# Graph attention stack on one core: a product moved to ScalarE as a biased exponential, the first norm written one step sooner, start and end rearranged

## The chip, the core and the metric

The kernel runs on one core of one Trainium2 chip. The engines of the core work from queues of their own, each in order: TensorE (PE in the profile, PEld for its weight loads), VectorE (DVE), ScalarE (ACT), GpSimd (POOL) and SyncE (SP, which here only issues DMA transfers). They wait for each other by semaphores. The metric is the time of one execution on the device in microseconds (us), as the median of several runs; the profile is of one further execution.

## The reference

The input `x` holds 32 batches of 512 nodes with 256 features, in float32; `adj` is a 512 x 512 adjacency matrix shared by all batches. Four layers follow, each added to its input:

- every layer starts with `h = max((x - mean) / sqrt(var + 1e-5), 0)` along the features;
- layers 0 and 1 are graph attention with one head: `Wh = h W`, `e_ij = leaky_relu(s_i + s_j)` masked by `adj`, softmax along j, the average of `Wh` with these weights, then elu (layer 0) or relu (layer 1);
- layer 2 is the same with four heads of 64 features;
- layer 3 is a linear map to 512 features, an attention over all nodes without a mask, a linear map back to 256, and a masked attention, with elu twice and residuals.

Since `leaky_relu(z) = max(z, alpha z)`, its exponential is the maximum of two products of a factor of i and a factor of j, so the kernel needs exponentials of the vectors `s_i` and `s_j` alone, and one maximum per pair of nodes.

## The kernel before

**Streams.** Four streams work on the batches in turn; stream i takes batches i, i+4, i+8 and so on. Each is a Python generator (`batch`, `layer0` to `layer3`) that yields the moment at which it wants to be taken up again, and the loop at the end of `fast` always continues the generator that is due first. That sets the order in which instructions are written. `after_us` computes the due time from TensorE work and a given number of us. The framework's planner then orders the written instructions on every engine, with an earlier written one going first where several are ready by its own timing; `keep_in_program_order` ties an instruction behind the one written before it on its engine. The order on each engine is fixed once the program runs.

**The norm** (`norm`, L262). For two blocks of 128 nodes: BN_STATS and BN_AGGR on VectorE (L268, L269), Ln of the variance and Exp of -0.5 times it on ScalarE (L271, L272), which gives `rs`, 1/deviation. Then VectorE writes `xn`: either the full norm (L279, `late` false: the first norm of a batch and that ahead of layer 3) or only `x` minus the mean (L275, ahead of layers 1 and 2), where `rs` is multiplied in behind the projection. `batch` (L729) takes a batch's tile, which was loaded a batch earlier, does the first norm on its four blocks, yields, and begins layer 0. `turned` (L291) transposes `xn` on TensorE (L70) and ScalarE copies it out with relu (L289). All streams share three `xn` buffers.

**The values** (`values`, L307). Per block of 128 nodes two matmuls (L66) give 256 features and 3 attention columns in a PSUM bank. In layers 0 and 3 ScalarE takes Exp of the 3 columns (L318) and then writes the features times the first of these (L319). In layer 1, with `rs`, ScalarE takes Exp of the columns scaled by `rs` (L321), VectorE multiplies `rs` with the first of them into `both` (L323), and ScalarE writes the features times `both` (L324), which frees the bank. While all streams are active a stream has two banks of its own.

**The weights** are written on VectorE (L352, one instruction per block of nodes), aggregation is matmuls of them with the values. Layer 3 avoids the full matrix for its unmasked attention by sorting: a scatter by indirect DMA (L606, issued by GpSimd), running sums on VectorE and TensorE (L626 to L647), and a gather (L654). The last batch does that attention directly instead (`attend`).

**The output step** (`layer3`, from L694): for two blocks at a time Exp and Relu of the averages (L698, L699), a second elu (L409 to L411), transposes of the residual, a sum (L709), Relu (L710), the sum with `x` on GpSimd (L712) and the store (L713).

**The start.** SyncE issues the load of the first `x`, then W0 and its attention vectors `a0`, `adj` fifth, and the rest. The vectors are scaled on VectorE (`scale_a`, L109), W0 is completed by three columns (`project`, copies at L126). `setup` turns `adj` into a mask: `own` (L209, L210), transposes, `maskT` (L219). A minimum over `adj` (L225), for a test of whether the fast form may be used, is written after that.

Of the kernel before, what the change touches and what calls it, by code (L numbers as in the profile page):

```python
# [28 lines left out]
P = 128  # L29
# [6 lines left out]
def fast(ctx, tc, flag, x, adj, w0, a0, w1, a1, w2, a2, mlp1_w, mlp1_b, mlp2_w, mlp2_b,  # L36
# [70 lines left out]
        return t  # L107

    def scale_a(t, alpha):  # L109
        nc.vector.tensor_scalar_mul(t[:, :, 1:2], t[:, :, 0:1], alpha - 1.0)  # L110
        nc.vector.tensor_scalar_mul(t[:, :, 2:3], t[:, :, 2:3], 1.0 - alpha)

    def project(dst, block, k, a_cols):

# [13 lines left out]
    def fetch_w(w, a, name):  # L128

        kt, cols = w.shape[0] // P, w.shape[1]  # L130
        t = const.tile([P, kt, cols + 3], FP, name=name)
        wr = w.rearrange("(k p) f -> p k f", p=P)
        for c in range(0, cols, F):
            nc.sync.dma_start(t[:, :, c + (3 if c else 0):c + (3 if c else 0) + F], wr[:, :, c:c + F])
        return t, fetch_a(a, name + "a")

    def finish_w(fetched, alpha):
        t, a_cols = fetched
# [8 lines left out]
            yield  # L147


    xts = {0: load_x(0)}  # L150
    W0, _ = fetched0 = fetch_w(w0, a0, "W0")
    adj_sb = work.tile([P, NT, N], I32, tag="w", name="adj", bufs=4)
    nc.sync.dma_start(adj_sb, adj.rearrange("(t p) j -> p t j", p=P))
    for b in range(1, NS):
# [51 lines left out]
    def setup():  # L206

        own = work.tile([P, NT, N], FP, tag="w", name="own", bufs=4)
        nc.vector.tensor_scalar(own, adj_sb, 0.0, None, op0=OP.is_gt)  # L209
        nc.gpsimd.affine_select(  # L210
            out=own, in_=own, pattern=[[P, NT], [-1, N]], base=0, channel_multiplier=1,
            compare_op=OP.not_equal, fill=1.0,
        )
        for j in range(NT):
            turn[0] = NS - 1 - j % (NS - 1)
            p = bank()
            for t in range(NT):
                transpose(p[:, t * P:(t + 1) * P], own[:, t, j * P:(j + 1) * P], ident, j + t == 0)
            nc.scalar.copy(maskT[:, j, :], p)  # L219
        turn[0] = NS - 1  # L220
        yield
        yield from finish_w(fetched1, 0.01)


        tc.keep_in_program_order(nc.vector.tensor_reduce(differ[:, 0:1], adj_sb, AX.XY, OP.min))  # L225
        nc.vector.tensor_scalar(differ[:, 0:1], differ[:, 0:1], 0.0, None, op0=OP.is_lt)
        least = small([1], "rden")
        nc.vector.tensor_reduce(least, diag, AX.X, OP.min)
        nc.vector.tensor_scalar(differ[:, 1:2], least, 0.0, None, op0=OP.is_le)
        nc.vector.tensor_copy(W2[:, :, :, :D], raw2.rearrange("p k (h d) -> p k h d", d=D))  # L230
        nc.vector.tensor_scalar_mul(A2v[:, :, 1:2], A2v[:, :, 0:1], -0.8)
        nc.vector.tensor_scalar_mul(A2v[:, :, 2:3], A2v[:, :, 2:3], 0.8)
        for k in range(KF):
            project(W2[:, k, :, D:], lambda k, f: raw2[:, k, f * P:(f + 1) * P], k, A2)
            yield
        yield from finish_w(fetched3, 0.2)

        for tri, sign in ((before, 1), (after, -1)):
            nc.vector.memset(tri, 1.0)
            nc.gpsimd.affine_select(  # L240
                out=tri, in_=tri, pattern=[[sign, P]], base=0, channel_multiplier=-sign,
                compare_op=OP.is_gt, fill=0.0,
            )
        ties = work.tile([P, 2 * N - P], FP, tag="w", name="ties", bufs=4)
        nc.vector.memset(ties, TINY)
        nc.gpsimd.affine_select(
            out=ties, in_=ties, pattern=[[-1, 2 * N - P]], base=N - P, channel_multiplier=1,
            compare_op=OP.is_gt, fill=0.0,
        )
        nc.vector.tensor_copy(band, ties)  # L250
        yield
        yield from finish_w(fetched4, 0.2)

    def small(shape, name):
        return work.tile([P] + shape, FP, tag=name, name=name, bufs=2 * NS)

    def new_xn():
        return work.tile([P, NT, F], FP, tag="xn", name="xn", bufs=3)  # L260

    def norm(xt, xn, rs, t0, late):  # L262


        st = small([2, 6], "st")
        mv = small([2, 2], "mv")
        for i in range(2):
            nc.vector.bn_stats(st[:, i, :], xt[:, t0 + i, :])  # L268
            nc.vector.bn_aggr(mv[:, i, :], st[:, i, :])  # L269
        rp = rs[:, t0:t0 + 2]  # L270
        nc.scalar.activation(rp, mv[:, :, 1], AF.Ln, bias=eps)  # L271
        nc.scalar.activation(rp, rp, AF.Exp, scale=-0.5)  # L272
        for i in range(2):
            if late:
                nc.vector.tensor_scalar(  # L275
                    xn[:, t0 + i, :], xt[:, t0 + i, :], mv[:, i, 0:1], None, op0=OP.subtract
                )
            else:
                nc.vector.tensor_scalar(  # L279
                    xn[:, t0 + i, :], xt[:, t0 + i, :], mv[:, i, 0:1], rp[:, i:i + 1], op0=OP.subtract, op1=OP.mult  # L280
                )
# [22 lines left out]
        c = next(noted)  # L304
        nc.vector.tensor_reduce(seen[:, c:c + 1], e, AX.XY, OP.max)

    def values(hT, w, rs=None):  # L307

        v = work.tile([P, NT, F + 3], FP, tag="v", name="v", bufs=4)
        for t in range(NT):  # L310
# [9 lines left out]
            else:  # L320
                nc.scalar.activation(v[:, t, F:], ps[:, F:F + 3], AF.Exp, scale=rs[:, t:t + 1])  # L321
                both = small([1], "both")
                nc.vector.tensor_tensor(both, rs[:, t:t + 1], pj, op=OP.mult)  # L323
                nc.scalar.activation(v[:, t, :F], ps[:, :F], AF.Copy, scale=both)  # L324
            if t + 1 < NT:
                yield after_us(0)
# [59 lines left out]
        nc.vector.reciprocal(r, den)  # L386
        return r

    def plain(hT, w, rs=None):
        v = yield from values(hT, w, rs)  # L390
        wt = weights(lambda t: v[:, t, F + 2:F + 3], lambda j: v[:, j, F + 1:F + 2])
        note(v[:, :, F:])
        yield after_us(3.2)
# [19 lines left out]
    def layer0(xt, xn, rs, when):  # L413
        v, wt = yield from plain((yield from turned(xn, when)), W0)
        xn, rs = new_xn(), small([NT], "rs")
        for t0 in range(0, NT, 2):
            r, q = pair(), pair("q")
            for i in range(2):
# [3 lines left out]
                if i == 0:  # L422
                    yield after_us(0)
            add_elu(xt[:, t0:t0 + 2, :], r, q)
            norm(xt, xn, rs, t0, True)
            last, when = when, after_us(6)
            if t0 == 0:
                yield after_us(0)
        yield last
        return xn, rs, when  # L430

    def layer1(xt, xn, rs, when):
        v, wt = yield from plain((yield from turned(xn, when)), W1, rs)
        xn, rs = new_xn(), small([NT], "rs")
        for t0 in range(0, NT, 2):
            r = pair()
# [252 lines left out]
    def layer3(xt, xn, when, b):  # L689
# [1 line left out]
        yield from (attend if b >= B - 1 else sort_attend)(oT, b)  # L691
        rT = yield from linear_t(oT, WM2, b2, "rT", 2)
        v, wt = yield from plain(rT, WHA)
        for t0 in range(0, NT, 2):  # L694
            y, q = pair(), pair("q")
            for i in range(2):
                p, rd = averages(v, wt, t0 + i)
                nc.scalar.activation(q[:, i, :], p, AF.Exp, scale=rd)  # L698
                nc.scalar.activation(y[:, i, :], p, AF.Relu, scale=rd)  # L699
                yield after_us(0)  # L700
            elu2_plus1(y, q)
            p = bank()
            for i in range(2):
                for k in range(KF):
                    transpose(
                        p[:, (i * KF + k) * P:(i * KF + k + 1) * P], rT[:, k, (t0 + i) * P:(t0 + i + 1) * P], ident
                    )
            yf = y.rearrange("p a f -> p (a f)")
            nc.vector.scalar_tensor_tensor(yf, p, -1.0, yf, op0=OP.add, op1=OP.add)  # L709
            nc.scalar.activation(y, y, AF.Relu)  # L710
            xr = xt[:, t0:t0 + 2, :]
            nc.gpsimd.tensor_tensor(xr, xr, y, op=OP.add)  # L712
            nc.sync.dma_start(  # L713
                out[b, t0 * P:(t0 + 2) * P, :].rearrange("(t p) f -> p t f", p=P), xr
            )
            yield after_us(0)

    def mlp_in(oT, y, t):
# [7 lines left out]
            o, p.rearrange("p (f c) -> p f c", c=P), -1.0, o, op0=OP.add, op1=OP.add  # L726
        )

    def batch(b):  # L729
        xt = xts.pop(b)  # L730
        xn, rs = new_xn(), small([NT], "rs")
        for t0 in range(0, NT, 2):
            norm(xt, xn, rs, t0, False)
        yield after_us(4)
        when = after_us(2)
        for layer in (layer0, layer1, layer2):
            xn, rs, when = yield from layer(xt, xn, rs, when)
# [479 lines left out]
```

## Time and profile before

| what | value |
|---|---|
| median of 3 runs | 2943.76 us (2943.12 to 2945.2) |
| the profiled execution's own time | 2945.59 us |
| its span, first to last instruction | 2943.9 us |
| mean granted TensorE clock | 0.995 |
| bytes moved by DMA | 270.89 MB |
| period of a batch in the middle of the run | 89.3 us |

In the lines below a group of a timeline reads: start and duration in us, engine, line of the kernel, operation, what it writes <- what it reads (buffer numbers left out), partitions x elements, number of instructions; in brackets how long the engine had been idle and what ended that. A line of the waits reads: who waited <- for whom, us in total, times, the longest. A line of a group reads: line, engine, operation, operands, count | us busy, mean ns of one | us idle before it and what ended that. A line of windows gives the busy time of each engine in that stretch.

### The profile page before, as it was taken

What the parts mean: (1) busy time and instruction counts of PE and PEld (TensorE: products, weight loads), DVE (VectorE), ACT (ScalarE), POOL (GpSimd) and SP (SyncE); (2) the same over time, 40 slices, a digit from 0 to 9 for tenths busy, and PEclk for the clock granted to TensorE, in tenths of its full rate; (3) what the DMA queues carried; (4) which work ended last, traced back from release to release, by engine and by line L of the source; (5) the groups of instructions that cost most, each with busy time, mean ns of one, the idle gap of its engine ahead of it and who ended that gap; (6) DMA issues with size and microseconds to landing.
All of it is one profiled execution on the core that took longest, in us unless ns stands there. A gap on an engine that the chain in (4) does not pass through costs nothing.

```text
span 2943.9 us, 43065 instructions
## 1 busy us (share of the span) xinstructions
PE 2863.2 (97%) x15177; PEld 2326.1 (79%) x15177; DVE 2224.0 (76%) x5674; ACT 1537.4 (52%) x3918; POOL 501.3 (17%) x509
## 2 busy tenths in 40 slices
PE   7999999999999999999999999999999999999988
PEld 6777888877887877888878888778888788887766
DVE  4677877778877778878777878777777788787764
ACT  4444455554555554555554555545555555555544
POOL 0011112111122111122021121121221111221120
PEclk9999999999999999999999999999999999999999
DMA  3033223233223233233332232332232322332230
GB/s 94 19 101 99 87 83 116 92 96 99 90 87 105 95 98 98 83 102 98 98 101 90 86 107 93 96 99 89 87 116 89 99 95 81 101 112 77 96 106 23
DMA packets 193150, 270.89 MB, mean 92 GB/s; under 512 B 16992, under 2 KB 156062, under 8 KB 192928
## 3 DMA queue, kind: packets, MB, share of 16 engines
q1 hardware_dynamic: 163168, 169.76, 18.5%
q0 software_dynamic: 29760, 98.30, 10.1%
q8 instruction: 123, 2.02, 0.3%
q14 instruction: 99, 0.81, 0.1%
HBM read 152.62 MB, written 115.39 MB: 91 GB/s over the span
## 4 chain that ended last, share of the span: by engine, by line
PE 77%; DVE 13%; ACT 5%; DMA 3%; issue 1%; POOL 0%; SPq 0%; POOLq 0%; ACTq 0%; DVEq 0%
PE b L66 70%; PE b L70 7%; DVE st L268 3%; DVE xn L279 1%; DMA order<-v,at 1%; DVE xn L275 1%; DVE sums L640 1%; DVE w L352 1%; ACT v L324 1%; DMA sums<-order 1%; DVE sums L631 1%; ACT y L504 1%; DVE x L405 1%; ACT q L503 1%; DVE y L404 1%
## 5 line engine op out<-in xcount | busy, mean ns | idle before, releaser
L66 PE MATMUL b<-v,w 128*128 128x65 f32 (+1 forms) x7232 | 1222.4, 321 | 6.8 <-DVE w L352 6.7
L66 PEld LDWEIGHTS b<-v,w 128*128 128x128 f32 x7232 | 1053.6, 192 | 167.8 <-issue 64.2
L66 PE MATMUL b<-WFC,oT 128*128 128x256 f32 (+1 forms) x2048 | 496.3, 380 | 0.0
L66 PEld LDWEIGHTS b<-WFC,oT 128*128 128x128 f32 x2048 | 373.6, 189 | 48.7
L66 PE MATMUL b<-W,hT 128*128 128x259 f32 (+1 forms) x1536 | 382.0, 387 | 9.2 <-ACT hT L289 4.4
L352 DVE SCALAR_TENSOR_TENSOR w<-b,v,maskT 128x512 f32<-128x512 f32 x512 | 369.0, 743 | 4.9 <-PE b L70 3.6
L606 POOL DMA_INDIRECT order<-v,at x248 | 284.2, 1146 | 491.2 <-DVE oT L725 152.0
L66 PEld LDWEIGHTS b<-W,hT 128*128 128x128 f32 x1536 | 283.0, 190 | 58.9 <-ACT v L324 8.9
L352 DVE SCALAR_TENSOR_TENSOR w<-spread,v,maskT 128x512 f32<-128x512 f32 x384 | 269.3, 741 | 0.0
L386 DVE RECIPROCAL rden<-b 128x1 f32<-128x1 f32 (+1 forms) x516 | 78.7, 164 | 246.5 <-PE b L66 243.2
L712 POOL TENSOR_TENSOR x<-x,y 128x512 f32<-128x512 f32 x64 | 81.3, 1270 | 1074.9 <-ACT y L710 963.8
L66 PE MATMUL b<-hT,WM 128*128 128x512 f32 x512 | 248.6, 596 | 0.7 <-ACT hT L289 0.7
L654 POOL DMA_INDIRECT g<-table,at x124 | 120.9, 975 | 724.8 <-ACT y L674 385.3
L66 PE MATMUL b<-oT,WM 128*128 128x512 f32 x512 | 230.3, 592 | 0.0
L528 ACT ACTIVATE v<-b,ends 128x256 f32<-128x256 f32 x256 | 118.6, 466 | 176.7 <-PE b L66 172.4
L268 DVE BATCH_NORM_STATS2 st<-x 128x6 f32<-128x256 f32 x512 | 192.7, 408 | 5.1 <-DMA x<-in_x_dram 2.6
L289 ACT ACTIVATE hT<-b 128x512 f32<-128x512 f32 x256 | 147.0, 590 | 83.8 <-PE b L70 83.8
L338 ACT ACTIVATE oT<-b,bias 128x512 f32<-128x512 f32 x128 | 87.7, 685 | 193.2 <-PE b L66 193.2
L411 DVE TENSOR_TENSOR y<-q,y 128x512 f32<-128x512 f32 x192 | 132.5, 690 | 67.0 <-ACT q L410 66.5
L70 PE MATMUL b<-ident,xn 128*128 128x128 f32 x1024 | 152.7, 279 | 23.5 <-DVE xn L279 20.9
L66 PEld LDWEIGHTS b<-oT,WM 128*128 128x128 f32 x512 | 97.0, 190 | 95.1 <-issue 91.8
L70 PEld LDWEIGHTS b<-ident,xn 128*128 128x128 f32 x1024 | 121.9, 143 | 60.6 <-DVE xn L279 33.8
(142 smaller groups left out, 3738.3 us busy)
## 6 DMA issues: line engine op xcount, KB each, us to landing
table<-sums SPq DMA_DIRECT2D x62, 1032.0 KB
sums<-order SPq DMA_DIRECT2D x62, 516.0 KB
spread<-row SPq DMA_DIRECT2D x96, 256.0 KB
x<-in_x_dram SPq DMA_DIRECT2D x32, 512.0 KB
out_dram<-x SPq DMA_DIRECT2D x64, 256.0 KB
sums<-order SPq DMA_DIRECT2D x62, 129.0 KB
order<-v,at POOLq DMA_INDIRECT x248
g<-table,at POOLq DMA_INDIRECT x124
```

What stands on the lines that cost most here:

```text
L66: nc.tensor.matmul(p, w, x, **flags)
L70: instruction = nc.tensor.transpose(p, x, i)
L268: nc.vector.bn_stats(st[:, i, :], xt[:, t0 + i, :])
L289: nc.scalar.activation(hT[:, :, t0 * P:(t0 + 2) * P], p.rearrange("p (k n) -> p k n", k=KF), AF.Relu)
L338: nc.scalar.activation(o[:, f, :], p, AF.Relu, bias=bias[:, f:f + 1])
L352: w = nc.vector.scalar_tensor_tensor(wt[:, j, :], r, t_col(j), maskT[:, j, :], op0=OP.max, op1=OP.mult)
L386: nc.vector.reciprocal(r, den)
L411: nc.vector.tensor_tensor(r, q, r, op=OP.add)
L528: nc.scalar.activation(halves[c][:, t, :F], ps[:, :F], AF.Copy, scale=ends[:, t, 0:1])
L606: nc.gpsimd.indirect_dma_start(out=orders[c], out_offset=bass.IndirectOffsetOnAxis(ap=at[:, 0, t:t + 1], axis=0), in_=halves[c][:, t, :], ...
L654: nc.gpsimd.indirect_dma_start(out=g, out_offset=None, in_=table, in_offset=bass.IndirectOffsetOnAxis(ap=at[:, 1, t:t + 1], axis=0),)
L712: nc.gpsimd.tensor_tensor(xr, xr, y, op=OP.add)
```

## The change

It has five parts.

- `values` in layer 1: `both` is no longer a product on VectorE but an Exp on ScalarE, of the first column scaled by `rs` with `ln` as its bias; `ln` is the logarithm of `rs`. For it `norm` in layer 0 keeps the Ln in a tile of its own, and GpSimd multiplies this by -0.5 in place, two columns at a time.
- The first norm of batch b + 4 is written in the output step of batch b, after its first pair of blocks, instead of after that step. Batches 0 to 3 have theirs at the start as before.
- The last batch does its output step with one block at a time instead of two, and its sum with `x` on VectorE; its stores are of one block each.
- At the start the two loads of `a0` are issued ahead of `x` and W0; the scaling of all attention vectors is on GpSimd; the minimum over `adj` and the test behind it are written directly behind `own`, tied there.
- The buffers of `st` go from eight to four.

```diff
     def scale_a(t, alpha):
-        nc.vector.tensor_scalar_mul(t[:, :, 1:2], t[:, :, 0:1], alpha - 1.0)
-        nc.vector.tensor_scalar_mul(t[:, :, 2:3], t[:, :, 2:3], 1.0 - alpha)
+        nc.gpsimd.tensor_scalar_mul(t[:, :, 1:2], t[:, :, 0:1], alpha - 1.0)
+        nc.gpsimd.tensor_scalar_mul(t[:, :, 2:3], t[:, :, 2:3], 1.0 - alpha)
...
+    a0_sb = fetch_a(a0, "W0a")
     xts = {0: load_x(0)}
-    W0, _ = fetched0 = fetch_w(w0, a0, "W0")
+    W0, _ = fetched0 = fetch_w(w0, a0_sb, "W0")
     adj_sb = work.tile([P, NT, N], I32, tag="w", name="adj", bufs=4)
     nc.sync.dma_start(adj_sb, adj.rearrange("(t p) j -> p t j", p=P))
...
             compare_op=OP.not_equal, fill=1.0,
         )
+        tc.keep_in_program_order(nc.vector.tensor_reduce(differ[:, 0:1], adj_sb, AX.XY, OP.min))
+        nc.vector.tensor_scalar(differ[:, 0:1], differ[:, 0:1], 0.0, None, op0=OP.is_lt)
         for j in range(NT):
...
         yield from finish_w(fetched1, 0.01)
 
-        tc.keep_in_program_order(nc.vector.tensor_reduce(differ[:, 0:1], adj_sb, AX.XY, OP.min))
-        nc.vector.tensor_scalar(differ[:, 0:1], differ[:, 0:1], 0.0, None, op0=OP.is_lt)
...
-    def norm(xt, xn, rs, t0, late):
-        st = small([2, 6], "st")
+    def norm(xt, xn, rs, t0, late, ln=None):
+        st = small([2, 6], "st", NS)
...
         rp = rs[:, t0:t0 + 2]
-        nc.scalar.activation(rp, mv[:, :, 1], AF.Ln, bias=eps)
-        nc.scalar.activation(rp, rp, AF.Exp, scale=-0.5)
+        lp = rp if ln is None else ln[:, t0:t0 + 2]
+        nc.scalar.activation(lp, mv[:, :, 1], AF.Ln, bias=eps)
+        nc.scalar.activation(rp, lp, AF.Exp, scale=-0.5)
+        if ln is not None:
+            nc.gpsimd.tensor_scalar_mul(lp, lp, -0.5)
...
                 nc.scalar.activation(v[:, t, F:], ps[:, F:F + 3], AF.Exp, scale=rs[:, t:t + 1])
                 both = small([1], "both")
-                nc.vector.tensor_tensor(both, rs[:, t:t + 1], pj, op=OP.mult)
+                nc.scalar.activation(
+                    both, ps[:, F:F + 1], AF.Exp, scale=rs[:, t:t + 1], bias=ln[:, t:t + 1]
+                )
                 nc.scalar.activation(v[:, t, :F], ps[:, :F], AF.Copy, scale=both)
...
         v, wt = yield from plain(rT, WHA)
-        for t0 in range(0, NT, 2):
-            y, q = pair(), pair("q")
-            for i in range(2):
+
+        n = 1 if b == B - 1 else 2
+        for t0 in range(0, NT, n):
+            y, q = pair()[:, :n, :], pair("q")[:, :n, :]
+            for i in range(n):
...
-            xr = xt[:, t0:t0 + 2, :]
-            nc.gpsimd.tensor_tensor(xr, xr, y, op=OP.add)
+            xr = xt[:, t0:t0 + n, :]
+            (nc.gpsimd if n == 2 else nc.vector).tensor_tensor(xr, xr, y, op=OP.add)
             nc.sync.dma_start(
-                out[b, t0 * P:(t0 + 2) * P, :].rearrange("(t p) f -> p t f", p=P), xr
-            )
+                out[b, t0 * P:(t0 + n) * P, :].rearrange("(t p) f -> p t f", p=P), xr
+            )
+            if t0 == 0 and b + NS < B:
+                first_norm(b + NS)
             yield after_us(0)
...
-    def batch(b):
+    normed = {}
+
+    def first_norm(b):
+
         xt = xts.pop(b)
         xn, rs = new_xn(), small([NT], "rs")
         for t0 in range(0, NT, 2):
             norm(xt, xn, rs, t0, False)
-        yield after_us(4)
+        normed[b] = xt, xn, rs
+
+    def batch(b):
+        if b < NS:
+            first_norm(b)
+            yield after_us(4)
+        else:
+            yield after_us(4)
+        xt, xn, rs = normed.pop(b)
         when = after_us(2)
```

## The prediction

> **What bounds the kernel now.** I read the page's busy times first, then TensorE's waits from 280 to 2760 us, then the timeline around each kind of wait.
>
> ```profile
> PE 2863.2 (97%) x15177; PEld 2326.1 (79%) x15177; DVE 2224.0 (76%) x5674; ACT 1537.4 (52%) x3918; POOL 501.3 (17%) x509
> ```
>
> TensorE is busy 2863.2 of 2943.9 us and the change takes no matmul away, so it can win only from the 80.7 us of TensorE idleness. By 100 us windows about 24 of them lie before 200 us and 23 after 2800. Between, this is nearly all:
>
> ```profile
> PE b L70 <- DVE xn L279: 16.4, 28, 1.0
> PE b L70 <- ACT v L324: 12.4, 28, 0.9
> PE b L66 <- ACT v L324: 3.4, 15, 0.3
> PE b L66 <- ACT v L318: 0.8, 1, 0.8
> ```
>
> 28 waits for L279, one per batch 4 to 31 and 89.3 us apart, are the first norm of a new batch; the L324 waits are layer 1's values held back by `both`.
>
> **Part 1, first norm a step sooner.**
>
> ```profile
> 1615.47 0.17 DVE L386 RECIPROCAL rden<-b 128x1 f32<-128x1 f32 x1 [0.68 <-PE b L66]
> 1618.93 0.17 DVE L386 RECIPROCAL rden<-b 128x1 f32<-128x1 f32 x1 [3.28 <-PE b L66]
> ...
> 1626.64 1.51 DVE L279 TENSOR_SCALAR xn<-x,mv,rs 128x256 f32<-128x256 f32 x4
> ...
> 1627.11 0.77 PE L70 MATMUL b<-ident,xn 128*128 128x128 f32 x4 [0.80 <-DVE xn L279]
> ```
>
> Today its VectorE work, some 3.3 us (four statistics, four aggregates, four L279), runs just as TensorE wants it, behind layer 1's norm. It is now written after the first half of the output step, whose L712 ran at 1616.10. In 1615 to 1620 VectorE is busy 0.70 of 5.00 us, so the work falls into a hole; nothing that TensorE waits for today is queued there. The input tile was loaded a period before (L95 at 1537.87). The step issues no DMA; in ScalarE's queue two short Ln and two Exp move with it, past that step's L698 and L699. The `xn` buffer is held some 10 us longer, but of its three buffers I count two in use at 1617 to 1629, this one included. Behind the transposes TensorE has ready WFC matmuls. Of 16.4 us I take **15**; ends 8 (half turns into another wait) and 16.4.
>
> **Part 2, `both` on ScalarE.**
>
> ```profile
> 1773.63 0.27 ACT L321 ACTIVATE v<-b,rs 128x3 f32<-128x3 f32 x1
> ...
> 1775.96 0.15 DVE L323 TENSOR_TENSOR both<-rs,v 128x1 f32<-128x1 f32 x1
> 1776.15 0.47 ACT L324 ACTIVATE v<-b,both 128x256 f32<-128x256 f32 x1 [0.17 <-DVE both L323]
> ...
> 1776.68 0.65 PE L70 MATMUL b<-ident,v 128*128 128x128 f32 x4 [0.90 <-ACT v L324]
> 1776.82 0.48 DVE L631 SCALAR_TENSOR_TENSOR sums<-sums,T 128x258 f32<-128x258 f32 x1
> 1777.35 0.70 PE L66 MATMUL b<-sums,after 128*128 128x258 f32 x2
> ```
>
> The product takes 0.15 us but queues on VectorE for 2 us here; over 128 tiles paired in order L324 starts 1.86 us after L321 at the median, 0.48 at the least. L324 also frees the PSUM bank for which TensorE waits. The whole wait is not won: the matmul behind needs L631, which ends at 1777.30, and VectorE is busy 4.67 of 5.00 us in 1595 to 1600 and all of 1600 to 1605, the same place in another period. Taking 128 x 0.145 = 18.6 us off VectorE moves this by some tenths a batch. Of 16.4 us (15.8 in the view and one wait of 0.5 at 259) I take **8**; ends 0 (VectorE is late next) and 16.4.
>
> The price on ScalarE: one more activation per tile.
>
> ```profile
> L321 ACT ACTIVATE v<-b,rs 128x3 f32<-128x3 f32 x128 | 33.1, 258 | 43.2 <-PE b L66 42.8
> L318 ACT ACTIVATE v<-b 128x3 f32<-128x3 f32 x256 | 43.3, 169 | 68.1 <-PE b L66 66.7
> ```
>
> The row nearest is L321, 0.258 us with one per-partition operand; L318 without one takes 0.169. The new one has two (scale `rs`, bias `ln`), so 0.258 + 0.089 = 0.35 us. The Trainium skill ("ScalarE: Activation LUTs", What ACT_TABLE_LOAD costs) puts some 93 ns on each such operand over 186 ns, an estimate of 0.37, with 93 ns of overlap between neighbours. It speaks against the change where VectorE is free: L321 to L324 becomes about 0.26 - 0.09 + 0.35 + 0.03 = 0.55 us, above today's least. By the row 128 x 0.35 = 45 us come onto ScalarE, by the rule 48, on an engine idle for 48% of the span: **0** on the path by either, since the median wait falls by 1.3 us. Without that cover each would cost its 0.25 us net, 32 us.
>
> The `ln` multiply goes to GpSimd: 64 at 0.19 us by the row L575 (128x8), 12 us, bounded below by nothing. The skill ("GPSIMD Engine Reference", Key points) says GpSimd and VectorE share their SBUF interfaces. The trace shows it: at 1623.80 two L275 take 1.43 us beside L712, where they take 0.72 otherwise. By the durations alone these multiplies cost 0; by the rule up to 12 us of held VectorE, of which a small part meets a wait of TensorE: I take **-1**; ends 0 and -4. What is behind one in GpSimd's queue is a scatter L606 or L712; were it late, the sort's sums and the output would follow.
>
> **Part 3, the start.**
>
> ```profile
> 23.47 2.28 DVE L225 TENSOR_REDUCE differ<-adj 128x1 f32<-128x2048 int32 x1
> 25.66 2.72 DVE L352 SCALAR_TENSOR_TENSOR w<-b,v,maskT 128x512 f32<-128x512 f32 x4
> ...
> 26.46 2.94 PE L66 MATMUL b<-v,w 128*128 128x257 f32 x6 [2.73 <-DVE w L352]
> ```
>
> L225 stands straight ahead of the first weights. Moved behind `own` (10.99 to 12.22) it falls into VectorE's idle time from 12.35 to 16.35: up to +2.2. If it gets ahead of the two W0 copies at 12.13, TensorE's first projection (12.43) loses 2 instead. In SyncE's queue the two `a0` loads pass x and W0: two issues of 0.49 us, so x lands near 5.4 instead of 4.4, and the first transposes are later, unless their tiny packets hold x up more. Against that `W0a`, landed at 6.96 and 8.32, no longer stops VectorE (1.02 and 0.75 us) and its scaling leaves that queue for GpSimd, which is idle till 12.29. `adj` is still issued fifth. The scaling of the other weights is off the path. I take **+2**; ends -2 and +4.
>
> **Part 4, the end.**
>
> ```profile
> 2931.90 0.17 DVE L386 RECIPROCAL rden<-b 128x1 f32<-128x1 f32 x1
> ...
> 2932.58 1.26 POOL L712 TENSOR_TENSOR x<-x,y 128x512 f32<-128x512 f32 x1 [11.57 <-ACT y L710]
> 2932.89 1.23 DVE L409 TENSOR_SCALAR q<-q 128x512 f32<-128x512 f32 x1 [0.17 <-ACT q L698]
> ...
> 2937.20 1.26 POOL L712 TENSOR_TENSOR x<-x,y 128x512 f32<-128x512 f32 x1 [3.36 <-ACT y L710]
> ```
>
> From the last reciprocal to the end of L712 are 6.56 us. With one block instead of two per step, by steps from start to start (now, then): to L698 0.51, 0.35; to L409 0.48, 0.50; to L410 1.27, 0.32 (its L409 no longer runs beside L712); to L411 0.82, 0.57; to L709 0.73, 0.41; to L710 0.78, 0.48; to the sum 0.71, 0.48; the sum 1.26, 0.37 (half of L443's 0.719). Together 6.56 and 3.48: 3.1, and 0.3 for half the bytes in the last store, which now takes 3.3 us. **+3.4**; ends 2 and 4. Two more stores are issued, the early ones under matmuls.
>
> **Sum.** 15 + 8 - 1 + 2 + 3.4 = 27.4 us: the span goes from 2943.9 to 2916.5, the profiled execution from 2945.59 to 2918.2. The median is 1.83 under that execution, so 2943.76 - 27.4 = **2916.4**.
>
> **Rivals.** *VectorE becomes the limit*: freed waits return as waits for L631 and L352, part 2 brings 0 and the start is a wash: 15 - 1 + 3.4 = 17 us, **2926**. For it speaks the full VectorE behind the L324 waits; against it, that most of them are 0.2 to 0.5 us with a transpose or projection ready behind.
>
> *The planner undoes it*: the queues are ordered by a planner (L239, written late, ran at 1.54 us), which may put the norm back or trade one wait for another in each period. Then the end alone counts: **2940**. The hole at 1615 speaks against it.
>
> *Slower, by one mechanism*: the `ln` multiply lands in GpSimd's queue behind a waiting L712. Layer 0's second Exp ended at 1673.98, layer 1's first L321 came at 1680.87; between scatters and the L712 at 1702.00 GpSimd stood idle for 38.14 us. Behind that L712 `ln` would come at 1703.5, and ScalarE, in order, would stop for some 20 us with every PSUM drain behind it, hence TensorE. Two such batches of 32 eat the gain (27.4/20 = 1.4); four give 2916 + 80 = **2996**. Against it: in that idle time `ln`'s inputs are ready long before L712's, so it should be queued first.
>
> **How the numbers follow.** Forecast 0.60, VectorE the limit 0.26, undone 0.07, slower 0.07. The forecast's own range is 2905 to 2925. The best ends, 16.4 + 16.4 + 4 + 4 = 41, give 2903; the worst without the slower rival, 8 + 0 - 4 - 2 + 2 = 4, give 2940, but seldom all at once: 2903 to 2934. A difference under 0.2% (5.9 us) cannot be told from no change; so faster 0.86, same 0.07, slower 0.07.
>
> **What the next profile would show.** Right: in 280 to 2760 us no L279 wait on TensorE above 2 us in total, the L324 ones at least halved, new waits below 12; L279 of the first norm near 1615 rather than 1626; 64 short GpSimd multiplies right after their Exp; L352's first weights before 24 us; about 3.5 us from the last reciprocal to the last sum. Wrong: long ScalarE waits for `ln`, or TensorE waits for L631, L352 or L275 that add up to what left.

## The result, and the profile after

The changed kernel takes **2933.38 us** (median of 10 runs, 2929.85 to 2941.15) against 2944.32 for the kernel before in the same comparison: a ratio of 0.9966, 95% interval 0.9958 to 0.9974. That is 10.9 us less; the forecast was 27.4 less, 2916.4. The range (2903 to 2934) just holds the time; the size of the gain was wrong. The profiled execution took 2932.65 us with a span of 2931.0.

The page's busy times, and TensorE's waits from 280 to 2760 us, of the changed kernel (the line numbers behind L110 have moved: L275 is now L279, L279 L283, L324 L330, L352 L358, L462 L469, L669 L676):

```profile
PE 2861.4 (98%) x15177; PEld 2332.1 (80%) x15177; DVE 2216.9 (76%) x5548; ACT 1564.4 (53%) x4050; POOL 531.9 (18%) x579
```

```profile
PE b L66 <- DVE w L358: 16.7, 29, 1.1
PE b L66 <- DVE v L469: 11.7, 7, 2.7
PE b L66 <- ACT y L708: 1.3, 7, 0.2
```

Both waits that the change went for are gone without a rest: 16.4 us for the norm and 15.8 for layer 1's values. Two others stand in their place: 16.7 us for the weights (L358) and 11.7 us for layer 2's values (L469), which TensorE never waited for in that stretch before. In all, 33.0 us of waits have become 29.7.

**The L469 wait.** The timeline of the changed kernel around the longest of the seven, by VectorE, GpSimd, SyncE and TensorE:

```profile
1530.18 0.72 DVE L676 SCALAR_TENSOR_TENSOR g<-g,ends 128x516 f32<-128x516 f32 x1
...
1534.22 0.95 POOL L661 DMA_INDIRECT g<-table,at  x1 [2.19 <-ACT y L681]
1534.28 0.38 SPq L95 DMA_DIRECT2D x<-in_x_dram  x1
...
1536.41 2.84 PE L66 MATMUL b<-W,hT 128*128 128x268 f32 x12
...
1540.74 0.76 DVE L676 SCALAR_TENSOR_TENSOR g<-g,ends 128x516 f32<-128x516 f32 x1 [3.53 <-DMA g<-table,at]
1541.42 0.87 DVE L469 SCALAR_TENSOR_TENSOR v<-b,rs,v 128x256 f32<-128x256 f32 x2
...
1541.95 4.41 PE L66 MATMUL b<-W,hT 128*128 128x268 f32 x11 [2.69 <-DVE v L469]
```

VectorE stands 3.53 us at the second L676, the product of the third gathered block, whose gather was issued at 1534.22. Behind it in the queue are the layer-2 values that would free TensorE's banks. The load of `x` (L95) goes out 0.06 us behind the gather. By the stretches' windows the TensorE clock then falls (columns: stretch, its length, PE busy, granted clock, DMA share, GB/s):

```profile
1541.00:1542.00 1.00, 0.05 (x1) 1.00 0.00 0
1542.00:1543.00 1.00, 1.00 (x3) 0.58 0.00 0
1543.00:1544.00 1.00, 1.00 (x4) 0.50 0.00 0
1544.00:1545.00 1.00, 1.00 (x3) 0.50 0.00 0
1545.00:1546.00 1.00, 1.00 (x5) 0.71 0.00 0
```

The four slow windows lose 0.42 + 0.50 + 0.50 + 0.29 = 1.71 us more. In this execution it happens again at 1900 us.

**The L358 wait**, the place that the prediction showed at 1776 before:

```profile
1772.23 0.49 DVE L638 SCALAR_TENSOR_TENSOR sums<-sums,T 128x258 f32<-128x258 f32 x1
...
1772.75 0.75 DVE L358 SCALAR_TENSOR_TENSOR w<-b,v,maskT 128x512 f32<-128x512 f32 x1
...
1773.41 0.48 DVE L638 SCALAR_TENSOR_TENSOR sums<-sums,T 128x258 f32<-128x258 f32 x1
...
1773.55 0.70 PE L66 MATMUL b<-v,w 128*128 128x257 f32 x2 [0.76 <-DVE w L358]
```

VectorE works without a pause through the sort's sums (L638), and the weights stand in between. The values are early now, and TensorE waits for the weights instead.

**Start and end.** `differ` has left its place ahead of the first weights, and the last step is short:

```profile
12.29 0.22 DVE L126 COPY W<-b 128x3 f32<-128x3 f32 x2
12.43 2.28 DVE L215 TENSOR_REDUCE differ<-adj 128x1 f32<-128x2048 int32 x1
...
24.32 2.73 DVE L358 SCALAR_TENSOR_TENSOR w<-b,v,maskT 128x512 f32<-128x512 f32 x4 [0.22 <-PE b L70]
...
25.13 2.65 PE L66 MATMUL b<-v,w 128*128 128x257 f32 x11 [0.84 <-DVE w L358]
```

```profile
2922.67 0.16 DVE L392 RECIPROCAL rden<-b 128x1 f32<-128x1 f32 x1
...
2926.04 0.42 DVE L721 TENSOR_TENSOR x<-x,y 128x256 f32<-128x256 f32 x1 [0.15 <-ACT y L719]
```

Of the signs named in the prediction, these came: no wait for the norm or for layer 1's values, the first norm's L283 near 1615, GpSimd's multiplies right behind their Exp (0.08 us at the median), the short end. "New waits below 12" did not: they are 29.7 us.

The weights start at 24.32 us instead of 25.66, so not "before 24", and TensorE waits 0.84 us for them instead of 2.73; from the last reciprocal to the end of the last sum it is 3.79 us instead of 6.56.

### The profile page after: what moved, and what is told of

The parts are those of the page before. It is cut to its first block, busy times and chain, and to the rows that moved or that the text cites. A ratio compares the mean times of both kernels' runs of the same rounds, so it can differ in the third digit from the quotient of the medians.

```text
span 2931.0 us, 43097 instructions
## 1 busy us (share of the span) xinstructions
PE 2861.4 (98%) x15177; PEld 2332.1 (80%) x15177; DVE 2216.9 (76%) x5548; ACT 1564.4 (53%) x4050; POOL 531.9 (18%) x579
## 3 DMA queue, kind: packets, MB, share of 16 engines
q0 software_dynamic: 29760, 98.30, 10.2%
## 4 chain that ended last, share of the span: by engine, by line
PE 82%; DVE 9%; ACT 4%; DMA 3%; issue 1%; SPq 0%; DVEq 0%; POOLq 0%; ACTq 0%
PE b L66 76%; PE b L70 7%; DMA g<-table,at 2%; DVE w L358 1%; DVE st L269 1%; DVE sums L647 1%; DVE sums L638 1%; DVE xn L283 1%; ACT hT L293 1%; ACT y L511 1%; ACT q L510 1%; DVE tot L652 0%; DVE x L411 0%; DVE g L676 0%; DVE y L410 0%
## 5 line engine op out<-in xcount | busy, mean ns | idle before, releaser
L66 PE MATMUL b<-W,hT 128*128 128x259 f32 (+1 forms) x1536 | 387.1, 390 | 18.1 <-DVE v L469 11.7
L358 DVE SCALAR_TENSOR_TENSOR w<-b,v,maskT 128x512 f32<-128x512 f32 x512 | 369.1, 745 | 5.2 <-PE b L70 4.1
L358 DVE SCALAR_TENSOR_TENSOR w<-spread,v,maskT 128x512 f32<-128x512 f32 x384 | 269.6, 742 | 0.0
L721 POOL TENSOR_TENSOR x<-x,y 128x512 f32<-128x512 f32 x62 | 87.7, 1414 | 836.0 <-ACT y L719 758.0
L417 DVE TENSOR_TENSOR y<-q,y 128x512 f32<-128x512 f32 (+1 forms) x194 | 132.9, 685 | 92.5 <-ACT q L416 56.7
L70 PEld LDWEIGHTS b<-ident,xn 128*128 128x128 f32 x1024 | 124.8, 143 | 32.8 <-issue 6.2
```

The source lines that it names most:

```text
L66: nc.tensor.matmul(p, w, x, **flags)
L70: instruction = nc.tensor.transpose(p, x, i)
L358: w = nc.vector.scalar_tensor_tensor(wt[:, j, :], r, t_col(j), maskT[:, j, :], op0=OP.max, op1=OP.mult)
L417: nc.vector.tensor_tensor(r, q, r, op=OP.add)
L721: (nc.gpsimd if n == 2 else nc.vector).tensor_tensor(xr, xr, y, op=OP.add)
```

## The experiments

The recorded expectations use letters. Theory A is the forecast's sum, each part for itself. Theory B is the rival of A for the part in question: for the first norm, that the gather collides with the load of `x` (called theory C from `load_later` on); for the product, that VectorE is full at that place (called theory V from `u3_scalar` on). Theory D is the order of VectorE's queue, explained below. The buffers of `st` are four in every run that has the product on ScalarE and eight in the others; they were not varied alone.

### The parts by themselves

`first_norm_alone`: the kernel before, with `first_norm` and its call in the output step.

```diff
+            if t0 == 0 and b + NS < B:
+                first_norm(b + NS)
...
```

> Only the first norm is written a step sooner; the rest is the kernel before (before: 2944.3 us). Theory A (the forecast's sum, each part for itself): the 16.4 us of TensorE waits for the norm go and nothing comes back, 2929 us (-15). Theory B (the gather collides with the load of x once the norm no longer stands ahead of it): the same 16.4 us go, but TensorE gets waits for layer 2's values behind VectorE's wait for the gather, 7 to 12 us in all at the same seven places as in the changed kernel, and one or two stretches at half clock in the middle; 2936 to 2941 us (-3 to -8).

2941.48 us against 2943.55, a ratio of 0.9992 (0.9984 to 1.0000). TensorE's waits, 280 to 2760 us:

```profile
PE b L66 <- DVE v L462: 14.2, 7, 3.1
PE b L70 <- ACT v L324: 9.2, 22, 0.9
PE b L66 <- DVE w L352: 4.8, 6, 0.8
```

The norm's waits go and 14.2 us for layer 2's values come, with three half-clock stretches that cost 1.71 us each (at 1899, 2257 and 2616 us). The first part makes this wait by itself.

`both_alone`: the kernel before with the product on ScalarE and the `ln` multiply on GpSimd.

```diff
-                nc.vector.tensor_tensor(both, rs[:, t:t + 1], pj, op=OP.mult)
+                nc.scalar.activation(
+                    both, ps[:, F:F + 1], AF.Exp, scale=rs[:, t:t + 1], bias=ln[:, t:t + 1]
+                )
...
```

> Only the product is made by ScalarE, with the GpSimd multiplies; the first norm stays late. Theory A: the L324 kind of TensorE wait (15.8 us) is at least halved and 7 us stay won: 2937 us. Theory B (VectorE is full at that place, so the wait only changes its name): TensorE's waits for the weights of a layer (16.7 us in the changed kernel) take the place of those for the values, 2942 to 2945 us (0 to -2). No wait for the gather above 1.5 us in either.

2949.81 us, a ratio of 1.0019 (1.0012 to 1.0026): **slower** by 6.3, worse than either theory.

```profile
PE b L66 <- DVE w L357: 19.3, 34, 1.2
PE b L70 <- DVE xn L282: 16.6, 28, 0.8
```

The 15.8 us for the values became 19.3 for the weights. In the profile the middle is 2.7 us longer and the start 7.5 (5.1 of them are half clock), while 5.4 come back behind 2774 us.

`norm_and_both`: both of them, start and end as before.

> Both middle parts, with start and end as before. Theory A: 2922 us (-22), and the missing gain must then come from the new start. Theory B: the middle of the changed kernel whole: 2934 to 2939 us (-5 to -10), TensorE's waits between 280 and 2760 us near 30 us, as in the changed kernel. If the 5.7 us that the changed kernel won between 2802 and 2932 us belong to the middle parts, they are here too.

2939.99 us, 0.9989 (0.9982 to 0.9997): -3.6, just under what theory B gives, far from A's -22. Its waits are 16.7 us for L357 and 12.3 for L468, those of the changed kernel.

`ends_alone`: the changed kernel with the first norm and the product put back, so parts 3 and 4.

> Only start and end are rearranged; norm and product as before. Forecast: -2 at the start and -3.4 at the end, 2939 us. From the trace of the changed kernel: the last step from reciprocal to sum 3.8 us instead of 6.6 (-3), the start 4 us sooner at 36 us and, if the half-clock stretches at 40 to 82 us are the start's own doing, nothing left of that by 200 us: 2941 us. If those stretches came from the first norm's new place, the 4 us stay: 2937 us.

2936.76 us, 0.9978 (0.9970 to 0.9986): -6.8. The number is the one given for a start that stays won, but the trace tells it otherwise: after 269 us of work it stands at 269.2. The last step brings 3.2 us, the time between 2774 and 2932 us 2.2, the middle 1.3.

### What holds VectorE at the gather

`load_later`: the changed kernel, the load of `x` moved behind the sort.

```diff
+        if b + NS < B:
+            xts[b + NS] = load_x(b + NS)
         rT = yield from linear_t(oT, WM2, b2, "rT", 2)
...
-        if b + NS < B:
-            xts[b + NS] = load_x(b + NS)
         yield from layer3(xt, xn, when, b)
```

> The changed kernel (2933.4 us) with the load of the input tile of batch b+4 issued after the sort step of batch b instead of before its layer 3, so that it no longer goes out within 0.3 us of the third gather. Theory C (the transfer collides): VectorE's wait for the third gather falls from 3.5 and 2.2 us to 1.5 us or less, TensorE's waits for layer 2's values from 11.7 us to 4 or less, the half-clock stretches in the middle go: 2921 to 2926 us. Theory D (the order of VectorE's queue, where the third gather's product stands ahead of all four layer-2 values in every fourth batch, is the cause, whatever the transfer meets): the seven waits stay above 8 us in sum, 2930 to 2936 us.

2936.05 us, 0.9977 (0.9967 to 0.9987) of before. The wait stays:

```profile
PE b L66 <- DVE w L358: 16.7, 29, 1.0
PE b L66 <- DVE v L469: 12.6, 7, 2.7
```

But this run does not test theory C, for the load did not move in time. Its timeline at the same place:

```profile
1529.75 0.95 POOL L661 DMA_INDIRECT g<-table,at  x1 [2.18 <-ACT y L681]
1529.82 0.38 SPq L95 DMA_DIRECT2D x<-in_x_dram  x1
```

Wherever it is written, the load waits for the store that frees its tile (27 times among SyncE's waits, `SPq L95 <- DMA out_dram<-x`). In all seven places it still goes out 0.05 to 0.29 us behind the third gather; in the kernel before it went out 3.3 to 4.0 us ahead of it.

The trace of the changed kernel speaks for a collision. By its DMA packets, the third gather's first packet comes 2.71 to 3.09 us after the issue in the 13 batches whose load goes out within 0.3 us of it, and 1.63 to 1.67 us after it in the other 17 (batches 0 to 29). Batch 28 is the next in the row of batches 4, 8 and so on to 24, but has no load left to issue: 1.65 us against their 2.71 to 2.91. So the load costs the gather some 1.2 us, an estimate from these numbers; without it the seven waits of TensorE (1.18 to 2.70 us) would come to about 3 us instead of 11.7. No run kept the load away from the gather, so this stays untested. Why two of the seven gathers end later still (5.8 and 6.0 us after the issue, the others 4.6 to 4.7) is open; theirs are the two waits over 2.5 us.

The order of the queue has its own part in the wait. VectorE's queue as built, in every fourth batch (seven in all; the products of the four gathered blocks are numbered):

```
before              changed kernel      third_in_order
product 1           product 1           product 1
...                 ...                 ...
values, block 0     product 3           values, block 0
values, block 1     values, block 0     values, block 1
product 3           values, block 1     values, block 2
values, block 2     values, block 2     values, block 3
values, block 3     values, block 3     product 2
product 2           product 2           product 3
```

Product 3 is placed ahead of product 2, in the kernel before as well: the tie on it only holds it behind what was written just before it on VectorE. The kernel before at this place:

```profile
1537.44 1.51 DVE L279 TENSOR_SCALAR xn<-x,mv,rs 128x256 f32<-128x256 f32 x4
1537.87 0.38 SPq L95 DMA_DIRECT2D x<-in_x_dram  x1
1538.88 0.75 DVE L669 SCALAR_TENSOR_TENSOR g<-g,ends 128x516 f32<-128x516 f32 x1
...
1541.57 5.53 PE L66 MATMUL b<-W,hT 128*128 128x268 f32 x24
1541.85 0.96 POOL L654 DMA_INDIRECT g<-table,at  x1 [6.23 <-ACT y L674]
...
1546.68 0.76 DVE L669 SCALAR_TENSOR_TENSOR g<-g,ends 128x516 f32<-128x516 f32 x1 [1.44 <-DMA g<-table,at]
```

Product 1 stood right behind the first norm (L279). VectorE stood 1.44 us at product 3 here too, but two of the four values were ahead of it, and TensorE went through its projection (x24) without a wait. With the norm gone, product 1 runs 6.2 us ahead of the projection instead of 2.7, and product 3 stands two values earlier, ahead of all four; so it is in `first_norm_alone`. Its gather can't start before ScalarE has read product 1, and is issued at 1534.22, only 3.3 us before ScalarE begins the first value's exponential (L468 at 1537.52). By what timing the planner chose this order is not on record.

`third_later`: the plain way, a later due time for products 2 to 4.

```diff
-            landed = after_us(3)
+            landed = after_us(6)
```

> The changed kernel with the due time of the second to fourth gather's product 6 instead of 3 us after the one before, nothing else; in VectorE's queue the third product then stands behind all four layer-2 values in every batch, and behind the second. Theory D: TensorE's waits for layer 2's values (11.7 us) and the half-clock stretches they bring (1.7 us each) go: 2918 to 2925 us (-8 to -15 against the changed kernel), unless the later products hold up the projection behind them. Theory C: the wait on the gather stays and only its victim changes, 2930 to 2936 us.

**3133.65 us**, 1.0645 (1.0627 to 1.0663). The L469 wait falls to 3.2 us as theory D says, and 200 us come in elsewhere; the granted clock falls to a mean of 0.958. The first of TensorE's waits in the middle:

```profile
PE b L66 <- DVE tot L635: 59.2, 13, 7.0
PE b L70 <- ACT ln L273: 26.6, 12, 3.6
PE b L66 <- DVE w L358: 25.9, 47, 3.8
```

By the loop at the end of `fast`, a due time does not only move one instruction: it delays its stream, and so changes how the four streams stand to each other. The run can't judge the theory. `third_later_u3`, the same with the edit below, had the same fate (3132.31 us):

> Both of the two last edits on the changed kernel. If each works and they are independent, the sum of their gains: 2912 to 2922 us. If neither does, 2931 to 2936 us.

`third_in_order`: only the order. The product is tied behind the product before it; `got` keeps both.

```diff
...
+            with tc.issue_after(got[-1][1]) if got else nullcontext():
+                mixed = nc.vector.scalar_tensor_tensor(z, z, ends[:, t, 2:3], g[:, 2 * C:], ...)
+            tc.keep_in_program_order(mixed)
...
```

On VectorE seven instructions move; the queues of the other four engines are the same to the last instruction.

> The changed kernel with the third gather's product tied behind the second's on VectorE, nothing delayed: in VectorE's queue seven instructions move, each from ahead of the four layer-2 values to behind them. Theory D (queue order): TensorE's 11.7 us of waits for layer 2's values fall to 2 or less, and the half-clock stretches at 1542 and 1900 us (1.7 us each) with them: 2917 to 2923 us. If the time is lost there in any case (the waits come back elsewhere, as they did before), 2929 to 2934 us.

**2915.49 us** (2914.77 to 2916.01), 0.9903 (0.9888 to 0.9918) of before: 17.9 us from seven places in a queue. Waits from 280 to 2760 us, and the timeline:

```profile
PE b L66 <- DVE w L358: 17.1, 29, 1.2
PE b L66 <- ACT y L708: 1.3, 7, 0.2
```

```profile
1528.11 0.95 POOL L661 DMA_INDIRECT g<-table,at  x1 [2.18 <-ACT y L681]
...
1530.31 5.53 PE L66 MATMUL b<-W,hT 128*128 128x268 f32 x24
...
1536.18 0.48 DVE L469 SCALAR_TENSOR_TENSOR v<-b,rs,v 128x256 f32<-128x256 f32 x1 [1.29 <-ACT v L468]
1536.58 0.74 DVE L676 SCALAR_TENSOR_TENSOR g<-g,ends 128x516 f32<-128x516 f32 x1
1537.44 0.74 DVE L676 SCALAR_TENSOR_TENSOR g<-g,ends 128x516 f32<-128x516 f32 x1
```

TensorE goes through layer 2's projection in one piece (x24 in 5.53 us); products 2 and 3 come after the values and wait for nothing. The load still goes out 0.05 to 0.14 us behind the gather in the seven places, so the order is enough to end the wait, whatever the load adds to it.

`before_in_order`: the same tie on the kernel before, to see whether it is an improvement of its own.

> The kernel before with the third gather's product tied behind the second's (seven instructions moved on VectorE, each from between the second and third layer-2 value to behind the fourth). If the 17.9 us were the change's own gain that the queue's order took back: nothing to win here, since TensorE has no wait for layer 2's values in the kernel before; 2941 to 2945 us. If the tie is an improvement by itself: 2926 to 2935 us.

2945.39 us, 1.0001 (0.9992 to 1.0010): nothing. So the 17.9 us are gain of the change itself, which the order had taken.

`first_norm_in_order`: the kernel before, the first norm a step sooner, and the tie.

> The kernel before with the first norm a step sooner and the tie, no other part of the change. If the queue's order is what ate the first part (it brought 2.1 us without the tie, with 14.2 us of waits for layer 2's values): those waits go and it brings 13 to 18 us, 2926 to 2931 us. If half of the norm's waits return elsewhere anyway: 2934 to 2938 us.

2921.16 us, 0.9922 (0.9906 to 0.9939): **-23.0**, more than the 13 to 18 expected. Its queues are those of `first_norm_alone` (-2.1) but for the seven instructions on VectorE.

### The limit on VectorE

`u3_scalar`: the changed kernel, one product of the sums on ScalarE.

```diff
-            nc.vector.tensor_scalar_mul(u[:, 3, :], u[:, 3, :], T[:, 3:4])
+            nc.scalar.activation(u[:, 3, :], u[:, 3, :], AF.Copy, scale=T[:, 3:4])
```

> The changed kernel with one product of the sort's sums (0.35 us, 62 of them) made by ScalarE instead of VectorE. Theory V (VectorE is full in the stretch where layer 1's weights are due, so the waits for the product became waits for the weights): TensorE's 16.7 us of waits for the weights fall by a quarter to a half, 4 to 8 us less time, 2925 to 2930 us. If those waits come from something else (their order in the queue, not the amount), nothing moves: 2931 to 2936 us.

2926.09 us, 0.9941 (0.9925 to 0.9958), so 7.3 us under the changed kernel as theory V gives, though the L358 wait falls by a fifth only (13.6 us in 22 waits) and the L469 wait is 13.4. The execution with the trace was the slowest of the four (2931.17), with 6.8 us of half clock in the middle, so by which waits the median fell is not shown.

`in_order_u3`: the tie and this edit together.

> That edit and the one product of the sort's sums on ScalarE. Independent: the gain of the tie plus the 7 us that the product brought, 2910 to 2916 us. If they fight for the same idle time: 2917 to 2923 us.

**2910.91 us**, 0.9889 (0.9874 to 0.9904), the best of all: 4.6 under `third_in_order`, 22.5 under the changed kernel.

`no_both_in_order`: `third_in_order` with layer 1's product back on VectorE.

> The changed kernel with the tie, and layer 1's product back on VectorE; third_in_order (2915.5 us) without the second part. If VectorE is the limit and nothing else relieves it, the second part only renames waits: 2914 to 2918 us. If it is worth the forecast's 8 us: 2922 to 2925 us.

2913.17 us, 0.9899 (0.9880 to 0.9918): not slower than with the second part (2915.49, at 0.9888 to 0.9918). Its waits are those for the values again:

```profile
PE b L70 <- ACT v L328: 9.2, 22, 0.9
PE b L66 <- DVE w L356: 4.7, 6, 0.8
PE b L66 <- ACT v L328: 3.5, 15, 0.3
```

19.0 us in this view with a last line of 1.6, 18.4 with the second part: it renames the waits.

`no_both_in_order_u3`: the same, with the sums' product on ScalarE.

> The kernel of the line before with layer 1's product put back on VectorE, so without the change's second part. If that part brings nothing since VectorE is the limit (as it brought -6 us alone and +1.5 beside the first part), within 3 us of the line before, either side. If it is worth the forecast's 7 us once the other waits are gone: 7 us slower than the line before.

2918.66 us, 7.8 slower than `in_order_u3` ("the line before" of the expectation), and 7.6 of them in the middle. So once VectorE has 0.35 us less in each sum, the second part is worth what the forecast gave it. In the table's stretch the four kernels with the tie take 2483.1 us with neither edit, 2481.4 with either one, and 2473.8 with both: each alone brings 1.7 us, the two together 9.3.

`in_order_u3_pool`: one more addition of the sums, on GpSimd.

```diff
-            nc.vector.tensor_tensor(sums[:, 2, 0, :], u[:, 0, :], u[:, 1, :], op=OP.add)
+            nc.gpsimd.tensor_tensor(sums[:, 2, 0, :], u[:, 0, :], u[:, 1, :], op=OP.add)
```

> The second kernel of this row with one addition of the sums (0.43 us on VectorE, 62 of them) on GpSimd as well. VectorE the limit: the waits for the weights fall again by 2 to 5 us, 2906 to 2913 us. If GpSimd holds VectorE up while it adds, or the sums come late to TensorE: no gain or 2 to 8 us slower than the second.

2918.68 us, 7.8 slower than `in_order_u3` ("the second kernel of this row"), 5.1 of them in the middle, with the L358 wait unchanged at 13.6 us. GpSimd is no relief here; whether the addition holds VectorE up or only comes late was not told apart.

### All in one table

The stretch of TensorE's work that the kernel before does between 269 and 2774 us, found in each trace by adding up the columns of its matmuls and transposes. Idle is the sum of the gaps ahead of matmuls, a stop a gap over 0.1 us, the rest is the time less the gaps; half clock is what the stretches below 0.97 lose, for the most part within the rest. Each row but its median is of one execution. The two kernels with the later due time are left out.

| kernel | median us | stretch | idle | stops | rest | half clock |
|---|---|---|---|---|---|---|
| before | 2944.3 | 2505.0 | 33.6 | 72 | 2471.4 | 0 |
| before_in_order | 2945.4 | 2503.9 | 32.8 | 72 | 2471.0 | 0 |
| first_norm_alone | 2941.5 | 2504.0 | 33.7 | 53 | 2470.3 | 5.1 |
| both_alone | 2949.8 | 2507.7 | 39.1 | 72 | 2468.7 | 0 |
| norm_and_both | 2940.0 | 2497.9 | 31.8 | 45 | 2466.1 | 1.7 |
| ends_alone | 2936.8 | 2503.7 | 32.5 | 71 | 2471.2 | 0 |
| changed kernel | 2933.4 | 2497.4 | 30.0 | 43 | 2467.5 | 3.4 |
| load_later | 2936.1 | 2498.4 | 31.0 | 43 | 2467.4 | 3.4 |
| u3_scalar | 2926.1 | 2496.7 | 29.1 | 37 | 2467.6 | 6.8 |
| first_norm_in_order | 2921.2 | 2481.2 | 18.1 | 44 | 2463.1 | 0 |
| no_both_in_order | 2913.2 | 2483.1 | 19.4 | 46 | 2463.6 | 0 |
| third_in_order | 2915.5 | 2481.4 | 18.7 | 36 | 2462.7 | 0 |
| no_both_in_order_u3 | 2918.7 | 2481.4 | 19.7 | 44 | 2461.7 | 0 |
| in_order_u3 | 2910.9 | 2473.8 | 14.9 | 29 | 2458.9 | 0 |
| in_order_u3_pool | 2918.7 | 2478.9 | 17.3 | 36 | 2461.6 | 0 |

## Why the prediction was wrong, step by step

**Where the 10.9 us come from.** The profiled executions differ by 12.9 us. By the same points of work the changed kernel stands, against before: +3.3 us at 269, -4.2 at 2774, -7.8 at 2841, -9.9 at 2932, -12.9 at the end.

**Part 1, the step that failed.** "Nothing that TensorE waits for today is queued there" looks at the place to which the norm goes, and held there:

```profile
1615.60 2.28 DVE L283 TENSOR_SCALAR xn<-x,mv,rs 128x256 f32<-128x256 f32 x4
```

No wait for the norm is left. The failed step is the price of 15 with a lower end of 8: it took every other instruction of VectorE's queue as staying where it was, and so put what would fill the place that the norm left at nothing. Product 1 moved up into it and product 3 with it, so that in every fourth batch four values came to stand behind a gather. That the step "issues no DMA" is true, but the third gather now goes out together with the load of `x`. TensorE waited 11.7 us for those values, 14.2 in first_norm_alone. By the table, first_norm_alone and first_norm_in_order differ by 2504.0 - 2481.2 = 22.8 us: 15.6 of idle, 5.1 of half clock, and 2.1 for nine stops less. The planner was named among the rivals, at 0.07, as trading one wait for another "in each period", and priced as giving back everything; it took back nearly all of the first part. With the queue in order the step is worth more than its 16.4 us of waits: 23.0. So the size of the term was wrong too, since each stop costs TensorE more than its gap (below).

**Part 2, mis-sized, and as the rival had it.** Forecast 8. Beside the first part in order it brought nothing (2915.49 with it, 2913.17 without it; 1.7 us in the table's stretch), and alone it made the kernel 6.3 us slower. The end "0 (VectorE is late next)" was the right one. The view that should have decided was in the prediction: VectorE busy 4.67 of 5.00 us at that place, with L631 right behind the product. That "most of them are 0.2 to 0.5 us with a transpose or projection ready behind" did not count, because the weights were late instead, in 34 waits of both_alone. The price on ScalarE held: 0.345 us for the 0.35 taken, and the features' product (L330) starts 0.585 us after the first exponential at the median, instead of 1.86. GpSimd's multiplies take 0.370 instead of 0.19 us at the median, and no engine that matters waits:

```profile
L327 ACT ACTIVATE both<-b,ln,rs x128: 337/345/363, 43.5 to 2752.0; 128x1 f32<-128x1 f32 x128
...
L276 POOL TENSOR_SCALAR ln<-ln x64: 215/370/1147, 37.3 to 2740.7; 128x2 f32<-128x2 f32 x64
...
  POOL order L613: 4.5, 4
```

These are lines of the view of the tile `ln`: least, median and longest ns, and in the last line who waited for it, us and times. The longest delay of a multiply behind its Exp is 3.96 us, so the rival of a multiply behind a waiting sum did not come. (One reading was off: a pair of L275 takes 0.60 us at the median in the kernel before, not 0.72; the 1.43 beside L712 stands.)

**Part 3.** Forecast +2; in the profile the start is 3.3 us longer. Half-clock stretches ahead of 269 us cost 5.1 us before and 8.5 after. Without them 269.0 and 272.3 become 263.9 and 263.8, and ends_alone, which has this part without the second, 269.2 - 6.8 = 262.4. That would be 1.5 us for the part, near its 2, but it is not shown: before_in_order has the start of the kernel before, instruction by instruction, and comes to 266.1 in the same way, which is 2.2 more. What is shown is that the first weights run 1.34 us sooner. Why the half-clock stretches fall as they do in the start is open; their cost differs between kernels that start alike (6.8 us in ends_alone, 1.7 in no_both_in_order).

**Part 4.** Forecast 3.4; it brought 3.0 us behind 2932 us, and from the last reciprocal to the last sum it is 3.79 us. Right.

**Not in the sum.** 5.7 us between 2774 and 2932, 3.6 of them around 2830. There TensorE waited 2.17 us for layer 3's values (L318) in the kernel before and then ran at half clock for 10.2 us, which cost 5.1. The wait is gone in the changed kernel, and in both_alone and first_norm_alone too; half clock between 2774 and 2932 us costs 1.7 us in each of the three, which would be most of the 3.6 us. What freed TensorE there was not singled out.

**The sum again.** With the queue in order, third_in_order brings 2943.67 - 2915.49 = 28.2 us against the forecast's 27.4. That agreement is partly luck: the first part is worth 23 instead of 15, the second next to nothing instead of 8. The range's lower part was right about what the change can bring, and the likeliest case wrong about what it brings as built.

## What to carry to other kernels

When work is moved out of an engine's queue, ask what the planner will put in its place: list the instructions behind it that wait for a DMA, and compare the two built queues around each before believing a sum of waits. If one stands wrong, tie that one by order; a changed due time moves the whole stream and can cost far more than the wait. A transfer that waits for its buffer is not moved by writing it elsewhere; look in the trace where it went. And taking a wait away is worth something only where the next thing needed is ready, which on an engine that is busy 4.67 of 5 us it is not.

## What the runs showed of the hardware

**A stop of TensorE costs more than its gap.** In the table 28 fewer stops (before to first_norm_in_order) save 15.5 us of idle and 8.3 of the rest, 0.30 each; 36 fewer (third_in_order) 8.7, 0.24 each. The trace of before shows where. After a stop for the norm, the first transpose is followed by the second 165 ns later, elsewhere 109 at the median; after a stop in a layer's projection the next matmul starts 323 ns later instead of 219. And the matmul ahead of the stop, 0.380 us long by its record where the next usually starts after 0.22, has no neighbour over its last 0.16 us, which is not counted as idle. That is 0.22 to 0.26 us a stop, an estimate, so the 28 waits of 16.4 us were worth about 23.

**Single waits of over 2.5 us mostly brought half clock.** Take the middle of the changed kernel, first_norm_alone, norm_and_both, load_later and u3_scalar. Of the eleven gaps over 2.5 us, ten have a stretch at 0.50 that begins between 0.6 us ahead of their end and 1.1 us behind it; it lasts 3.41 us and costs 1.71 (once 6.83 and 3.41). One gap, of 2.57 us, has none. Of the gaps of 1.0 to 1.8 us none has one; the only gap in between, of 1.87 us, has. The Trainium skill ("TensorE: Matmul & The Clock Gate", Part 1: The HAM clock gate) has the clock halved after an idle window of about 3.4 us, with windows that run freely. The length of the slow stretches agrees; that a gap shorter than a window can do it, but not always, is what these runs add.

**A gather issued together with a load started later.** Its first packet came 2.71 to 3.09 us after the issue instead of 1.63 to 1.67, in the changed kernel; the numbers and the one batch without a load stand under `load_later` above.
